# A two-layer kernel whose whole body is put into a block that the scheduler orders by a playback of time lines

## The chip, the core and the metric

The kernel runs on one core of one Trainium2 chip. The metric is the device time of one launch in microseconds. The time before is the median of 15 runs, 1619.65 us, with a lowest run of 1613.36 us and a highest of 1627.61 us.

## The reference, cut to what matters

The input is 8 sequences of 512 tokens with 128 features (4096 tokens). Two layers are computed. In each, the tokens are normalised, one branch `s` and one gate `g` are computed from the normalised tokens, and `x + s * silu(g)` goes on.

```python
xn = _layernorm(x)
s = _L0_attn_ref(xn, ...)   # a state-space block: convolution, scan over 512 steps, gating, MLP
g = _silu(_L0_ffn_ref(xn, ...))   # 24 experts, two matmuls with a layer norm between them
x = x + s * g
xn = _layernorm(x)
s = _L1_attn_ref(xn, ...)   # causal attention, 8 heads of 128
g = _silu(_L1_ffn_ref(xn, ...))   # 128 experts, one matmul each
x = x + s * g
```

The scan is `h = dA * h + dBx; y = h . C` over 512 steps, for 256 channels with 16 states each. The experts of both layers take the two best tokens' choices with a limited number of places; rows are moved to and from the experts by indirect DMAs. The second layer needs both branches of the first, sequence by sequence.

## The kernel before, in words

All of it is one function, `tile_kernel`, that traces about 10,000 instructions in program order. A list scheduler then decides the order on each engine: it walks through the traced instructions on a simulated machine and gives each engine, whenever it is free there, the ready instruction that comes first in program order. On the chip every engine then works through its own list in that fixed order; an instruction that waits holds back all that stand behind it on its engine. So the lists decide what may run beside what.

The work, in program order, with the names and lines that are used below:

- **prepare** (lines 230 to 282): for each sequence, layer norm, transposes, the router's logits and the running counts of the 24 experts. **routing** (lines 337 to 421) turns them into the places of the rows. The last step of it are the copies at lines 407 to 410, which hold the row numbers (`inv`) that the first expert gather needs.
- **expert1** (lines 439 to 455), 24 times: gather rows (`xg`), transpose, matmul (`ph`, line 453), scale, write to `hs_dram`.
- **between** (lines 457 to 504), 16 pairs of token tiles: gather four blocks (`hd`), add, layer norm (DVE lines 484 to 501), write to `hid_dram`.
- **expert2** (lines 506 to 522), 24 times: three gathers (`hg`), transposes (`pht`, line 515), matmul (`po`, line 520), scale, write to `os_dram`. Its first gather needs every row of `between`.
- **fetch** and **after** (lines 524 to 548): gather-add of `os_dram`, layer norm, gate; the input of the second layer for one sequence. The first of them needs every row of `expert2`.
- **front** (lines 551 to 586), **scan** (lines 591 to 632), **gate**, **back** (lines 635 to 704): the state-space block of one sequence. `scan` has 8 passes of two states each. Such a pass is called a *chunk* below; there are 64, numbered 0 to 63 through all sequences. A chunk is, for each half of the channels, two exponentials on ScalarE (ACT, line 603), a product on VectorE (DVE, line 605), two scans on DVE (line 607), a product on DVE (line 608), and 16 transposes on TensorE (PE, line 629) that add into PSUM. Its two broadcast loads (`bb`, `cb`, lines 597 and 598) are issued from ACT's queue.
- **Attention** (lines 743 to 914): `prepare` and `route` of one sequence, then `heads`, 8 passes. Such a pass is called a *head*; there are 64, numbered 0 to 63. Its scores are lines 849 to 864 (PE, a custom DVE reduction, an ACT exponential), its values lines 866 to 895 (transposes, a copy `pT` at line 879, matmul `po` at line 884, DVE sums at 893 and 895). The copies at lines 843 and 879 are written as `nc.any.tensor_copy`: the scheduler chooses DVE or ACT for each.
- **slots, experts, finish** (lines 954 to 998): the second layer's experts and the output.

In program order these parts are interleaved by hand: `step()` takes one chunk of the state-space block, and the calls of `step()` are spread over expert1, between, expert2 and the first 48 heads. Which chunk stands beside which expert or head on an engine is then the scheduler's choice. The PSUM pool `ps_m` (two buffers of tag `pm`) serves front, gate, back and, up to the end of the state-space block, the attention as well.

```python
    step()
    due = 0.0
    for n, of in mixture():
        due += n / of
        while due > 0.5:
            step()
            due -= 1.0
```

Of the kernel before, what the change touches and what calls it, by code (L numbers as in the profile page):

```python
# [42 lines left out]
)  # L43


@with_exitstack
def tile_kernel(ctx: ExitStack, tc: tile.TileContext, t: dict, out: bass.AP):
    nc = tc.nc
    V, S, G, T, Q = nc.vector, nc.scalar, nc.gpsimd, nc.tensor, nc.sync

# [5 lines left out]
    def load(src, shape, name, pool=None, dtype=F32):  # L56
# [11 lines left out]
        out=tri, in_=ones, pattern=[[1, P]], compare_op=ALU.is_gt, fill=0.0, base=0, channel_multiplier=-1  # L68
# [79 lines left out]
    def pool(stack, name, bufs, side, **more):  # L148
# [68 lines left out]
        out=group, in_=group, pattern=[[-B, H0]], compare_op=ALU.is_ge, fill=0.0, base=0, channel_multiplier=1  # L217
    )
    G.affine_select(
        out=group, in_=group, pattern=[[B, H0]], compare_op=ALU.is_ge, fill=0.0, base=B - 1, channel_multiplier=-1  # L220
# [3 lines left out]
        out=earlier, in_=earlier, pattern=[[-B, H0], [0, B]], compare_op=ALU.is_ge, fill=0.0, base=0,  # L224
# [438 lines left out]
    def back(b, yt):  # L663
# [49 lines left out]
        out=mask[:, L - P :], in_=mask[:, L - P :], pattern=[[-1, P]], compare_op=ALU.is_ge, fill=-FMAX,  # L713
# [512 lines left out]
```

## Time and profile before

| | |
|---|---|
| median of 15 runs | 1619.65 us |
| profiled execution, its own time | 1623.98 us |
| its span (first to last instruction) | 1622.3 us, so 1.7 us lie around it |
| DVE busy | 1257.7 us, 78% of the span |
| PE busy | 1233.2 us, 76% |
| ACT busy | 985.4 us, 61% |
| POOL (GpSimd) busy | 603.0 us, 37% |
| DMA | 222.76 MB, mean 137 GB/s |
| granted TensorE clock, mean | 0.873 |

The table is of the profiled execution, which is 4.3 us above the median. A busy share is the time in which the engine had at least one instruction in work, over the span. No engine is full on the average, so the order of the work in time matters beside its amount; the profile's busy shares over slices of time show where an engine is full.

### The profile page before, as it was taken

The numbers are of one execution on the slowest core, as the hardware profiler recorded it, in microseconds if no ns is written. First come the engines' busy times: TensorE is split into PE (matmuls) and PEld (weight loads), VectorE is DVE, ScalarE is ACT, GpSimd is POOL, SyncE is SP. The second block draws the span as 40 slices with busy tenths as digits, with TensorE's granted clock in tenths as the row PEclk, the third lists the DMA queues.
The fourth block names the chain that finished last, engine by engine and source line by source line (L and its number), as shares of the span: only waits on it lengthen the run. The fifth ranks groups of instructions, "written<-read, shape, count | busy, mean of one in ns | idle before, by whom it ended". The sixth has DMA issues, their size and how long they took to land.

```text
span 1622.3 us, 20522 instructions
## 1 busy us (share of the span) xinstructions
PE 1233.2 (76%) x6797; PEld 866.5 (53%) x6797; DVE 1257.7 (78%) x2831; ACT 985.4 (61%) x1696; POOL 603.0 (37%) x502
## 2 busy tenths in 40 slices
PE   4787989311388998254887898889979899898974
PEld 3653545101276886142465665666657667566743
DVE  6548686679856766695999999999999997475565
ACT  2226778566566786454677776767768665563363
POOL 2006763556283550723243503632430130210176
PEclk9887999655589999577798999989999999999987
DMA  5428987777567863423231321423211120058344
GB/s 139 152 95 295 308 284 234 225 234 246 166 214 235 264 198 136 112 77 85 72 107 46 104 90 34 114 77 97 63 57 66 53 71 1 28 148 240 94 111 122
DMA packets 170668, 222.76 MB, mean 137 GB/s; under 512 B 15722, under 2 KB 115898, under 8 KB 170562
## 3 DMA queue, kind: packets, MB, share of 16 engines
q1 hardware_dynamic: 125634, 101.35, 20.0%
q0 software_dynamic: 26496, 52.98, 12.4%
q10 hardware_dynamic: 18432, 67.12, 12.3%
q8 instruction: 54, 0.88, 0.2%
q14 instruction: 52, 0.43, 0.1%
HBM read 163.52 MB, written 57.80 MB: 136 GB/s over the span
## 4 chain that ended last, share of the span: by engine, by line
PE 34%; DVE 31%; DMA 12%; issue 9%; ACT 7%; POOL 6%; SPq 0%; ACTq 0%; POOLq 0%; DVEq 0%
DVE u L607 7%; PE sc L857 3%; PE po L884 3%; DVE u L605 3%; DVE u L608 3%; PE py L629 3%; DVE sc L859 3%; PE po L520 3%; PE ph L453 2%; DMA hd<-hs_dram,row 2%; DVE s L895 2%; PE pc L561 2%; POOL hd L127 2%; DVE pT L879 2%; PE pqm L849 1%
## 5 line engine op out<-in xcount | busy, mean ns | idle before, releaser
L607 DVE TENSOR_TENSOR_SCAN u<-da,u 128x512 f32<-128x512 f32 x256 | 311.1, 1235 | 68.8 <-ACT da L603 68.6
L629 PE MATMUL py<-ident,u 128*128 128x128 f32 x1024 | 170.2, 305 | 158.8 <-DVE u L608 158.6
L629 PEld LDWEIGHTS py<-ident,u 128*128 128x128 f32 x1024 | 135.4, 157 | 199.2 <-DVE u L608 177.2
L603 ACT ACTIVATE da<-dt,a_neg 128x512 f32<-128x512 f32 x256 | 175.7, 720 | 52.1 <-DVE u L607 49.7
L884 PE MATMUL po<-v,pT 128*128 128x129 f32 x1280 | 184.2, 286 | 23.8 <-DVE s L895 19.8
L884 PEld LDWEIGHTS po<-v,pT 128*128 128x128 f32 x1280 | 166.8, 198 | 56.1 <-issue 32.7
L863 ACT ACTIVATE prob<-sc,mn 128x128 f32<-128x128 f32 (+3 forms) x256 | 130.4, 527 | 98.4 <-DVE mn L859 90.6
L857 PE MATMUL sc<-xaT,qm 128*128 128x128 f32 (+3 forms) x512 | 179.5, 459 | 12.2 <-ACT prob L863 10.4
L605 DVE TENSOR_TENSOR u<-bb,lp 128x1024 f32<-128x1024 f32 x128 | 154.8, 1226 | 22.4 <-DMA bb<-xd_dram 16.7
L608 DVE TENSOR_TENSOR u<-u,cb 128x1024 f32<-128x1024 f32 x128 | 157.7, 1232 | 1.1
L859 DVE CUSTOM_DVE_ANT_0 sc<-sc,mask 128x128 f32<-128x128 f32 (+3 forms) x256 | 124.6, 494 | 31.9 <-PE sc L857 30.0
L127 POOL DMA_INDIRECT xg<-xn_dram,inv x72 | 98.0, 1361 | 121.5 <-DVE lp L584 79.4
L831 POOL DMA_INDIRECT xs_dram<-xn,idx x64 | 80.9, 1265 | 159.6 <-DVE idx L825 110.6
L877 PE MATMUL pp<-ident,prob 128*128 128x128 f32 x640 | 112.8, 284 | 27.3 <-DVE pT L879 21.6
L130 POOL DMA_INDIRECT o<-os_dram,row x64 | 113.7, 1776 | 47.6 <-DMA o<-xn_dram 29.8
L127 POOL DMA_INDIRECT hg<-hid_dram,inv x72 | 93.8, 1303 | 98.7 <-PE pht L515 48.5
L877 PEld LDWEIGHTS pp<-ident,prob 128*128 128x128 f32 x640 | 80.5, 145 | 89.2 <-issue 34.3
L857 PEld LDWEIGHTS sc<-xaT,qm 128*128 128x128 f32 x512 | 83.1, 198 | 50.3 <-ACT prob L863 28.4
L127 POOL DMA_INDIRECT hd<-hs_dram,row x64 | 76.0, 1188 | 76.6 <-DMA sb<-s_dram 30.8
L520 PE MATMUL po<-we,hgT 128*128 128x128 f32 x576 | 79.2, 286 | 0.3 <-ACT hgT L517 0.3
L520 PEld LDWEIGHTS po<-we,hgT 128*128 128x128 f32 x576 | 71.8, 198 | 11.8 <-issue 7.1
L849 PE MATMUL pqm<-xaT,m_qk 128*128 128x512 f32 x128 | 71.8, 652 | 4.5 <-DVE zm L701 1.9
(293 smaller groups left out, 2563.9 us busy)
## 6 DMA issues: line engine op xcount, KB each, us to landing
bb<-xd_dram ACTq DMA_DIRECT2D x64, 512.0 KB
cb<-xd_dram ACTq DMA_DIRECT2D x64, 512.0 KB
hs_dram<-hs SPq DMA_DIRECT2D x24, 768.0 KB
we<-in_W SPq DMA_DIRECT2D x48, 256.0 KB
hid_dram<-hd SPq DMA_DIRECT2D x32, 256.0 KB
we<-in_we SPq DMA_DIRECT2D x16, 512.0 KB
os_dram<-os SPq DMA_DIRECT2D x24, 192.0 KB
xb<-in_x SPq DMA_DIRECT2D x16, 256.0 KB
```

Of the source, the lines that this page charges most:

```text
L127: G.indirect_dma_start(dst, None, table[:, :], IOA(idx, 0))
L520: T.matmul(po[:, c, :], hT[:, f, :], we[:, f, :], start=False, stop=(f == NJ - 1))
L603: S.activation(da[:, j, :], dt[:, hf, :], AF.Exp, scale=a_neg[:, hf, n0 + j : n0 + j + 1])
L605: V.tensor_tensor(u, bb, bc(dx[:, hf : hf + 1, :], (P, NC, L)), ALU.mult)
L607: V.tensor_tensor_scan(u[:, j, :], da[:, j, :], u[:, j, :], 0.0, ALU.mult, ALU.add)
L608: V.tensor_tensor(u, u, cb, ALU.mult)
L629: T.matmul(py[:, i, hf * P : (hf + 1) * P], us[hf][:, j, i * P : (i + 1) * P], ident, is_transpose=True, start=False, stop=(n0 + j == DS - ...
L857: T.matmul(sc[:, :w], qm[:, i * P : w], xaT[:, :w], start=True, stop=True)
L859: V.tensor_tensor_reduce(sc[:, :w], sc[:, :w], mask[:, L - w :], -1.0, FMAX, ALU.add, ALU.min, mn[:, i : i + 1])
L863: S.activation(pr, sc[:, :w], AF.Exp, bias=mn[:, i : i + 1], scale=-1.0)
L877: T.transpose(pp[:, c, :], prob[i][:, k * P : (k + 1) * P], ident)
L884: T.matmul(po[:, i - i0, :], pT[:, i * (i + 1) // 2 + k, :], v[:, k, hd % 4, :], start=(k == 0), stop=(k == i),)
```

## The change

The old body of `tile_kernel` becomes a function `stages`, and `tile_kernel` calls it inside `tc.block(schedule_with_timeline_sim=True)`. The list scheduler then walks through the same traced instructions on another simulated machine, which plays back a time line for each engine and queue; so instructions become ready at other moments of that walk, and the lists come out in another order. Every tile and every computing instruction is the same; the engine of a `nc.any` copy is chosen anew.

```diff
+def tile_kernel(tc: tile.TileContext, t: dict, out: bass.AP):
+    with tc.block(schedule_with_timeline_sim=True):
+        stages(tc, t, out)
+
+
 @with_exitstack
-def tile_kernel(ctx: ExitStack, tc: tile.TileContext, t: dict, out: bass.AP):
+def stages(ctx: ExitStack, tc: tile.TileContext, t: dict, out: bass.AP):
     nc = tc.nc
```

Below, "the built order" is the list of instructions of each engine in the built program, before and after. Lines are those of the kernel before; in the changed kernel they are five higher.

## The prediction

> **What bounds the kernel now.** I read the page's busy shares over slices first, then the busy time of each engine by stage, then where the scans (line 607) and the attention matmuls (line 884) fall in these stages, and last the costliest groups. The page, with the engines' totals, slices, and the chain that ended last:
>
> ```profile
> PE 1233.2 (76%) x6797; PEld 866.5 (53%) x6797; DVE 1257.7 (78%) x2831; ACT 985.4 (61%) x1696; POOL 603.0 (37%) x502
> ...
> PE   4787989311388998254887898889979899898974
> ...
> DVE  6548686679856766695999999999999997475565
> ...
> PE 34%; DVE 31%; DMA 12%; issue 9%; ACT 7%; POOL 6%; SPq 0%; ACTq 0%; POOLq 0%; DVEq 0%
> ```
>
> DVE and PE have almost the same total, and neither is full. The slices show that they are full at different times, DVE from slice 20 to 33, PE in most others. Busy time by stage (window, length, then PE, PEld, DVE, ACT, POOL with instructions, granted clock, DMA share, GB/s):
>
> ```profile
> 0.00:133.00 133.00, 87.44 (x450) 59.66 (x450) 74.73 (x334) 34.08 (x53) 22.87 (x51) 0.85 0.48 147
> 133.00:313.00 180.00, 151.19 (x612) 83.86 (x612) 136.47 (x142) 130.47 (x212) 105.43 (x80) 0.91 0.82 269
> 313.00:440.00 127.00, 25.89 (x112) 21.08 (x112) 107.49 (x185) 78.51 (x126) 59.24 (x50) 0.52 0.68 216
> 440.00:650.00 210.00, 184.19 (x1329) 155.71 (x1330) 139.79 (x139) 150.87 (x287) 96.45 (x75) 0.93 0.65 207
> 650.00:811.00 161.00, 82.48 (x339) 51.57 (x337) 124.32 (x195) 85.03 (x130) 63.22 (x42) 0.71 0.32 87
> 811.00:1347.00 536.00, 476.43 (x2589) 333.84 (x2587) 513.76 (x1294) 377.53 (x653) 174.04 (x120) 0.95 0.25 74
> 1347.00:1423.00 76.00, 70.64 (x387) 48.67 (x386) 43.15 (x149) 40.79 (x82) 9.17 (x11) 0.98 0.10 29
> 1423.00:1622.00 199.00, 154.90 (x988) 112.11 (x986) 118.01 (x401) 88.07 (x156) 72.64 (x75) 0.90 0.51 140
> ```
>
> The stages are: start, expert1, between, expert2, the step to the first head, heads with scan, heads alone, tail. In the longest one, 811 to 1347, DVE is busy 513.76 of 536 us and PE 476.43: both are nearly full because scans and attention run beside each other. The same windows for the scans of line 607 alone (DVE busy, count) and the matmuls of line 884 alone (PE, PEld):
>
> ```profile
> 440.00:650.00 210.00, 61.88 (x52) 0.93 0.65 207
> ...
> 811.00:1347.00 536.00, 118.84 (x96) 0.95 0.25 74
> ```
> ```profile
> 811.00:1347.00 536.00, 120.06 (x841) 109.18 (x842) 0.95 0.25 74
> ```
>
> A chunk has four such scans, so 13 chunks lie beside expert2 and 24 beside the heads. The groups that price this:
>
> ```profile
> L607 DVE TENSOR_TENSOR_SCAN u<-da,u 128x512 f32<-128x512 f32 x256 | 311.1, 1235 | 68.8 <-ACT da L603 68.6
> L605 DVE TENSOR_TENSOR u<-bb,lp 128x1024 f32<-128x1024 f32 x128 | 154.8, 1226 | 22.4 <-DMA bb<-xd_dram 16.7
> L608 DVE TENSOR_TENSOR u<-u,cb 128x1024 f32<-128x1024 f32 x128 | 157.7, 1232 | 1.1
> L127 POOL DMA_INDIRECT hg<-hid_dram,inv x72 | 93.8, 1303 | 98.7 <-PE pht L515 48.5
> L879 DVE COPY pT<-pp 128x512 f32<-128x512 f32 x31 | 21.1, 680 | 2.4 <-PE pp L877 2.1
> L879 ACT COPY pT<-pp 128x384 f32<-128x384 f32 x60 | 28.7, 478 | 25.7 <-PE pp L877 25.4
> ```
>
> A chunk costs DVE (311.1 + 154.8 + 157.7) / 64 = 9.7 us.
>
> **How I price an order.** Nothing computes less, so I count what stands where in the built order after, and give each instruction the mean busy time of its group (line, shape, engine) in the trace before, overlap with its predecessor left out. Summed over the old order this gives back the page's totals. In a stage where engines feed each other, the time is at least the largest engine sum of the stage. Check on the old order: from head 0 to head 63, head by head, the largest sums add to 781 us; the trace has 790 (811 to 1601). Over the four stages from 133 to 811 us they add to about 155 + 121 + 197 + 128 = 601, against 678 (113%).
>
> **Part 1, the block itself.** The built program has one more branch on no engine and no barrier in the body: priced at nothing. At most it is one more wait of all engines; the 1.7 us around the span bounds that.
>
> **Part 2, the copies.** Of the `nc.any` copies DVE keeps 29 instead of 130 and ACT does 227 instead of 126. DVE loses 28 v copies at 682 ns, 53 pT of 384 columns at 545 and 20 of 512 at 680: 61.6 us, 55 without overlap. ACT gains 28 at 588, 53 at 478, 20 at 586: 53.5 us, and loses 32 of its 202 table loads at 1283 ns: 41 us; net 12. On a DVE-bound stretch the 55 us would be gain; the end values are 0 and -55.
>
> Taken alone, the Trainium skill (Perfetto Trace Analysis, Identifying the Most-Contended Engine) says to take the engine of highest occupancy, here DVE, and relieve that first; by it the profiled time would be 1624 - 55 = 1569 us. The same page (Optimization Strategy) says that a kernel whose most-contended engine changes over time can gain from interleaving these regimes; by it an order that parts them loses, and the rest of this text measures how much.
>
> **Part 3, the scan runs ahead of the experts.** In the old order, expert 0's matmul (line 453) stands beside chunk 1 and the last of expert1 beside chunk 11; between lies beside chunks 13 to 17, expert2 beside 18 to 30. In the new order DVE is done with chunk 0 after 61 us of work instead of 79, and routing is strewn among chunks: its last copy (line 408) stands behind 231 us of DVE work, at chunk 15. So expert1 runs beside chunks 16 to 31, between starts at chunk 34, and after chunk 39 the lists hold no scan until the first attention preparation: nine of the 16 pairs of between, then all 720 PE instructions of expert2 in one row, are alone. Front's second half for sequence 5, without which chunk 40 cannot start, stands behind that preparation. Stage by stage:
>
> - Chunk 0 done: 133 us before, of which DVE works 75; 18 us of DVE work and 16 us of PE work now stand behind it, and both fed it: 115.
> - Chunks 1 to 15 with prepare and routing: DVE 170 us. Chunks 0 to 4 ran at 97% in the trace, so 1.07 times: 182, to 297.
> - Expert1 with chunks 16 to 31: PE 180, DVE 175, ACT 154. Three full engines that feed each other had 180/155 before; I take 1.1: 198, to 495.
> - Chunks 32 to 39 and seven pairs: DVE 119, times 1.07: 128, to 623.
> - Nine pairs alone: DVE has 37 us, but the first eight pairs took 59 us in the trace with DVE not full (four gathers and two stores each), 7.4 a pair: 66, to 689.
> - Expert2 alone: PE 112 us, POOL 72 gathers at 1.303 = 94. Lead-in of the first gather 12, then 118: 819. DVE and ACT's scan work, 140 us of DVE in the old stage, is not there: this is the loss.
> - Fetch, after, preparation to head 0: 161 us before, with 124 of DVE work in it, and about 48 from preparation to head 0 alone. Now 8 gather-adds at 1.86 apart, then the chain: 60, to 879.
>
> Head 0 thus comes at about 879 us instead of 811, with the same 40 chunks done: +68.
>
> **Part 4, scans and heads part.** From there the old order has the last 24 chunks spread over 42 heads. In the new one chunks 40 to 47 stand beside heads 0 to 3, none beside heads 4 to 14, 48 to 55 beside 15 to 17, none to 28, 56 to 63 beside 28 to 31, none from there on. Largest sums: 95 (DVE), 139 (PE; DVE 81), 77 (DVE), 127 (PE; DVE 87), 72 (DVE), 148 (PE, heads 31 to 48). That is 658, where the old order needed 1423 - 811 = 612 in all; at 107% it is 704. The tail from head 48 has the same work as before: 199. Together 903. Head by head the largest sums are 865 against 781, which by the check is 875 from head 0 to 63, plus 21 after it: 896. So +85 to +92 here, the 55 us of Part 2 already in.
>
> **Part 5, other queues.** SP: fetch 0's load of `s_dram` now stands ahead of routing's copies to `inv` and waits for back 0; back 0 ends by chunk 12, `inv` needs chunk 15, so that hides it; if not, each us goes to expert 0. ACT issues the 128 loads of `bb` and `cb`; waits for `bb` were 16.7 us in all and lie in the 1.07; from none to one of the 7 us landings seen at some chunks, for each of the three bursts' eight, it is 0 to 168, and I stay at the row's 16.7. POOL's gathers keep their order, with two 1.28 us additions of back moved past.
>
> **Sum.** 879 + 896 = 1775, with the 1.7 around it 1777, less 4.3 (profiled run to median) 1772. Without any friction it is 115 + 170 + 180 + 119 + 66 + 112 + 60 = 822 to head 0 and 658 + 199 = 857 after it, or 835 if engines may drift by two heads: 1655 to 1677. Windows of four heads give 786 us for the new order and 727 for the old, so 786 x 790/727 + 21 = 875 after head 0 and 1751 in all. I take 1755.
>
> **Rivals.** (a) DVE's relief decides: the bursts hide, buffers let PE run past them, and the stretch 811 to 1347 falls to PE's 476 us at 97%, 490: 46 us less, 1575 us, faster. For it: DVE 96% busy there. Against: head 4's DVE instructions stand behind chunk 47 in one list. It wins only while head 0 comes less than 46 us late and the heads stay beside the scans. Chance 0.06. (b) The engines drift more than I allow, at or just under the frictionless sum: 1640 to 1677. Chance 0.14. (c) A queue blocks: loads at the burst starts, or an SP wait ahead of `inv`: 50 to 168 us on top, 1820 to 1930. Chance 0.1. (d) The order hardly changes, so no change: the built orders differ in over 4000 lines on PE, so 0.02. Forecast: 0.68.
>
> **How the numbers follow.** About 0.2% (3 us) is what a measurement can tell from no change. Faster: (a) and nothing else, 0.06; same: (d) and the edge between, 0.03; slower 0.91. The range leaves out (a), (d) and the upper part of (c), and reaches to (b): 1645 to 1845.
>
> **What would show it.** In the profile after: scans (x count of line 607) absent while line 520 runs, DVE near zero there for about 120 us; expert1 starting near 290 us; head 0 near 870 us; DVE copies at 879 down to 26; three DVE-full bursts between PE-full stretches. It is wrong if expert2 ends before 720 us, or if heads 0 to 63 take under 800 us.

## The result and the profile after

The changed kernel takes 1760.47 us (median of 9 runs, 1756.83 to 1766.91) against 1619.65 us (47 runs): a ratio of 1.0872, 95% interval 1.0853 to 1.0891, so 141 us slower. The forecast was 1755 us. The span of the profiled execution is 1759.2 us, the mean granted clock 0.843 against 0.873. Lines of the changed kernel are five higher than those named so far.

The page after, in the same lines as shown of before (totals, slices, chain):

```profile
PE 1249.8 (71%) x6797; PEld 890.3 (51%) x6797; DVE 1218.6 (69%) x2730; ACT 991.9 (56%) x1765; POOL 607.3 (35%) x502
...
PE   5863588989844119933666889669778799989960
...
DVE  7499998979798750004889637995388967455663
...
PE 14%; DVE 8%; ACT 4%; issue 4%; POOL 3%; DMA 2%; ACTq 0%; DVEq 0%; SPq 0%; POOLq 0%
```

The work is nearly the same: PE has 17 us more (1%), DVE 39 us less (3%). What is new is in the slices: three zeros in DVE's row at slices 16 to 18, and further on dips (6, 3, 5, 3) where DVE had nines. The chain holds 35% of the span only, so nothing is read from it. Busy time by stage (length, then PE, PEld, DVE, ACT, POOL with instructions, granted clock, DMA share, GB/s):

```profile
95.00:287.00 192.00, 115.34 (x599) 89.60 (x600) 182.77 (x238) 90.10 (x135) 34.41 (x14) 0.68 0.38 126
...
650.00:765.00 115.00, 110.12 (x936) 104.35 (x936) 0.00 (x0) 63.26 (x144) 66.22 (x70) 0.97 0.79 249
765.00:861.00 96.00, 31.25 (x76) 13.82 (x77) 40.87 (x127) 34.36 (x54) 79.02 (x59) 0.57 0.31 59
861.00:960.00 99.00, 63.17 (x299) 47.56 (x298) 89.58 (x192) 65.55 (x114) 40.53 (x22) 0.79 0.30 78
960.00:1090.00 130.00, 112.87 (x590) 76.80 (x589) 77.14 (x247) 80.08 (x140) 35.99 (x33) 0.95 0.18 50
1090.00:1185.00 95.00, 66.48 (x343) 45.78 (x341) 93.41 (x154) 55.01 (x108) 0.13 (x1) 0.89 0.21 72
1185.00:1307.00 122.00, 104.83 (x528) 69.13 (x529) 68.36 (x239) 73.23 (x138) 26.80 (x23) 0.93 0.16 42
1307.00:1409.00 102.00, 80.07 (x406) 56.28 (x405) 93.79 (x160) 72.34 (x129) 10.72 (x10) 0.87 0.21 70
1409.00:1554.00 145.00, 135.40 (x801) 99.31 (x800) 87.37 (x337) 91.33 (x176) 20.42 (x25) 1.00 0.14 40
```

The first line is DVE full with scans while no expert has begun. The second is expert2 with no DVE instruction at all; the third is the step to head 0. Then bursts of scans (DVE 90 of 99 us, PE 63) take turns with stretches of heads (PE 113 of 130, DVE 77). Head 0 stands here at its first value matmul (line 884): 811 us before, 861 now. For the kernels of the experiments it is its first sum (line 889), which comes 1 to 6 us later.

The granted clock is lower, but it cannot hold the loss: after head 0 PE is busy 705 us at a clock of 0.90 against 702 us at 0.94, so its work takes 3 us longer there, where the part itself grows from 811 to 898 us; in the whole kernel PE has 17 us more, against 137 us of span (before, then after):

```profile
811.00:1620.00 809.00, 701.97 (x3961) 494.62 (x3958) 674.92 (x1842) 506.39 (x890) 255.85 (x206) 0.94 0.30 86
```
```profile
861.00:1759.00 898.00, 704.99 (x3949) 501.92 (x3947) 625.14 (x1715) 524.17 (x966) 206.80 (x188) 0.90 0.26 73
```

The scans alone (line 612) from 861 us on, and the longest DVE wait between 640 and 870 us (total, times, longest):

```profile
861.00:960.00 99.00, 27.80 (x24) 0.79 0.30 78
960.00:1090.00 130.00, 9.29 (x8) 0.95 0.18 50
1090.00:1185.00 95.00, 37.22 (x32) 0.89 0.21 72
1185.00:1307.00 122.00, 0.00 (x0) 0.93 0.16 42
```
```profile
DVE lno_st L111 <- DMA o<-os_dram,row: 159.5, 13, 141.1
```

DVE stands once for 141.1 us: the layer norm of `after` heads its list and waits for rows that exist only when expert2 is done. The group of the scans:

```profile
L612 DVE TENSOR_TENSOR_SCAN u<-da,u 128x512 f32<-128x512 f32 x256 | 300.4, 1213 | 0.2
```
A scan costs what it did (1213 ns, 1235 before). Its engine waits for it less, 0.2 us against 68.8. In turn ACT, whose exponentials feed the scans, now waits 127.8 us for DVE's scans (49.7 before): the scans stand in blocks in which DVE is the late one, and between these blocks DVE has none.

### The profile page after: what moved, and what is told of

Its sections match the earlier page's. It is cut to its first block, busy times and chain, and to the rows that moved or that the text cites. A ratio compares the mean times of both kernels' runs of the same rounds, so it can differ in the third digit from the quotient of the medians.

```text
span 1759.2 us, 20610 instructions
## 1 busy us (share of the span) xinstructions
PE 1249.8 (71%) x6797; PEld 890.3 (51%) x6797; DVE 1218.6 (69%) x2730; ACT 991.9 (56%) x1765; POOL 607.3 (35%) x502
## 5 line engine op out<-in xcount | busy, mean ns | idle before, releaser
L612 DVE TENSOR_TENSOR_SCAN u<-da,u 128x512 f32<-128x512 f32 x256 | 300.4, 1213 | 0.2
L608 ACT ACTIVATE da<-dt,a_neg 128x512 f32<-128x512 f32 x256 | 170.5, 714 | 152.0 <-DVE u L612 127.8
L862 PE MATMUL sc<-xaT,qm 128*128 128x128 f32 (+3 forms) x512 | 197.2, 480 | 53.2 <-ACT prob L868 49.8
L634 PEld LDWEIGHTS py<-ident,u 128*128 128x128 f32 x1024 | 148.2, 171 | 169.7 <-DVE u L613 146.2
L132 POOL DMA_INDIRECT xg<-xn_dram,inv x72 | 127.7, 1774 | 81.5 <-DVE lp L589 32.5
L111 DVE BATCH_NORM_STATS2 lno_st<-o 128x6 f32<-128x128 f32 x32 | 9.3, 292 | 189.2 <-DMA o<-os_dram,row 189.1
L135 POOL DMA_INDIRECT o<-os_dram,row x64 | 105.8, 1654 | 51.3 <-DMA os_dram<-os 20.2
L882 PE MATMUL pp<-ident,prob 128*128 128x128 f32 x640 | 110.1, 283 | 15.2 <-ACT pT L884 10.8
L884 ACT COPY pT<-pp 128x384 f32<-128x384 f32 (+1 forms) x166 | 85.0, 512 | 63.7 <-PE pp L882 49.9
L132 POOL DMA_INDIRECT hd<-hs_dram,row x64 | 85.8, 1341 | 81.3 <-DVE u L612 22.4
L704 POOL TENSOR_TENSOR zm<-zm,b 128x512 f32<-128x512 f32 x8 | 33.0, 4121 | 229.2 <-PE pzt L690 160.2
L836 POOL DMA_INDIRECT xs_dram<-xn,idx x64 | 67.7, 1058 | 106.0 <-DVE row L833 84.0
```

The lines of the kernel that those rows point to most:

```text
L132: G.indirect_dma_start(dst, None, table[:, :], IOA(idx, 0))
L135: G.indirect_dma_start(dst, None, table[:, :], IOA(idx, 0), compute_op=ALU.add)
L608: S.activation(da[:, j, :], dt[:, hf, :], AF.Exp, scale=a_neg[:, hf, n0 + j : n0 + j + 1])
L612: V.tensor_tensor_scan(u[:, j, :], da[:, j, :], u[:, j, :], 0.0, ALU.mult, ALU.add)
L634: T.matmul(py[:, i, hf * P : (hf + 1) * P], us[hf][:, j, i * P : (i + 1) * P], ident, is_transpose=True, start=False, stop=(n0 + j == DS - ...
L862: T.matmul(sc[:, :w], qm[:, i * P : w], xaT[:, :w], start=True, stop=True)
```

## The experiments

The twelve kernels ran on three chips on which the kernel before has medians of 1640.93, 1641.05 and 1643.13 us, 1.3 to 1.5% above the 1619.65; so each result is read by its ratio to before on the same chip. Stage times come from one profile each, and against the two profiles above they carry that percent.

### The block alone

```diff
+def tile_kernel(tc: tile.TileContext, t: dict, out: bass.AP):
+    with tc.block():
+        stages(tc, t, out)
```

> The body in a block, but ordered as before, without the playback of time lines; the built order is the same as before on every engine, with one more branch. If the lost time comes from the order alone: 1620 us, within 4 us of before. If the block itself costs (a barrier, a branch, another start): up to the 1760 us of the changed kernel.

Measured: 1641.86 us, ratio 1.0003 (0.9968 to 1.0038). Without the playback the built lists are the old ones on every engine, and the time is the old one. All of the loss comes from what the playback changes: the lists, and the engines of the copies.

### Holding one instruction per chunk in program order

The first: from the end of expert2 on, the first product of each chunk and the first reduction of each head on DVE. The second: up to the end of expert2, the first transpose of each chunk on PE. The third: both.

```diff
-                V.tensor_tensor(u, bb, bc(dx[:, hf : hf + 1, :], (P, NC, L)), ALU.mult)
+                m = V.tensor_tensor(u, bb, bc(dx[:, hf : hf + 1, :], (P, NC, L)), ALU.mult)
+                if pin["dve"] and hf == 0:
+                    tc.keep_in_program_order(m)
...
+                        if pin["pe"] and hf == 0 and j == 0 and i == 0:
+                            tc.keep_in_program_order(m)
...
+                if pin["dve"] and i == 0:
+                    tc.keep_in_program_order(m)
```

> The changed kernel, but from the end of expert2 on the first DVE product of each chunk and the first DVE reduction of each head are held in program order on DVE, so that the remaining chunks are spread over heads 0 to 48 again. Experts and chunks before are left as changed (expert2 still alone, beside no chunk). Theory (two separate losses, experts late and scans parted from heads): head 0 stays near 860 us, the rest falls from 898 to about 820 to 840, 1680 to 1705 us. Rival (the time after head 0 is set by the sum of work and the copies on ACT, not by the spread): no change, 1750 to 1765 us. Rival (all of the loss is the late experts): no change either, with head 0 at 860.

> The changed kernel, but up to the end of expert2 the first PE transpose of each chunk is held in program order on PE, so that a chunk stands beside the expert it was written beside (expert 0 beside chunk 1, expert2 beside chunks 17 to 30). Scans and heads stay parted as changed. Theory: head 0 falls from 861 to about 810 to 825 us, the rest stays near 898, 1707 to 1725 us. Rival (the loss is the parting of scans and heads alone; the wait in expert2 costs nothing since the same 40 chunks are done): 1755 to 1765 us. Rival (all of the loss is the late experts): 1620 to 1640 us.

> Both holds at once: chunks beside their experts on PE, and beside their heads on DVE; the copies stay mostly on ACT (19 on DVE instead of 130 before). Theory: both losses go, 1620 to 1650 us; if the 60 us of copies taken off DVE are worth something in the DVE-full stretch, 1590 to 1615. Rival (something else in the order costs, such as POOL, SP or ACT's queue): above 1660 us.

Measured: ratios of 1.126 (1.1201 to 1.1319), 1.0988 (1.0926 to 1.1049) and 1.12 (1.1146 to 1.1254). Each hold made the changed kernel slower, so the two theories failed; of the third expectation its rival is left, that something else in the order costs. The second did bring expert1 forward, to 183 us from 287, and head 0 still came late, at 901. DVE's waits in the second, from 95 to 352 us, and in the first, from 888 to 1573 us:

```profile
DVE u L612 <- PE py L638: 69.7, 7, 28.2
```
```profile
DVE rsum L902 <- PE po L897: 57.8, 40, 6.2
```

In the second, the product of a chunk (line 605, here 612) waits for late transposes on PE, which have to read a buffer before it is written again. In the first, a sum of attention heads DVE's list while PE has not made its product. That wait is not new: it is 50.5 us in the changed kernel (861 to 1554) and 8.7 in the kernel before (811 to 1427). The hold did spread the scans, 12 to 16 in each 100 us from 888 to 1488 (15 to 21 in the kernel before), and the part after head 0 still takes 956 us: scans spread on DVE's list alone don't bring the time back. The third run has both sides of this: expert1 begins at 182 us, head 0 comes at 893, and the part after it takes 948. A chunk's first instruction was put back, while the playback ordered its partners on the other engines by its own time lines. So "chunks stand at the wrong heads" is not the whole cause; which list stands against which must be asked.

### One order up to head 0, the other after it

Here both programs' built lists are written into the kernel before, as a chain on every engine, and the engine of each copy as a letter. One kernel takes the old lists up to the first attention matmul (line 849) and the new ones from there, the other the reverse.

```diff
+    copies = iter(COPIES)
...
-                nc.any.tensor_copy(pT[:, first : first + n, :], pp[:, :n, :])
+                copy(pT[:, first : first + n, :], pp[:, :n, :])
...
+        for a, b in zip(places, places[1:]):
+            tc.add_manual_dep(
+                traced[b], traced[a].name,
+                mybir.DependencyInfo(mybir.DependencyClass.NoSync, mybir.DependencyReason.DATA),
+                reason="order",
+            )
```

> Every engine runs the kernel before's order up to the first attention head (copies on the same engines as there), and the changed kernel's order from there on. Two separate losses (theory A): head 0 where the kernel before has it, about 811 us, and after it the 898 us of the changed kernel: about 1710 us against 1620, some 5.5% more than before. One loss only at the front, the attention being slow because it starts late (theory B): after it about 811 us, the whole within 1.5% of before. The order is not what matters but the number of instructions and waits the frame makes (theory C): no clear figure, but both this kernel and its opposite would then be alike.

> Every engine runs the changed kernel's order up to the first attention head, and the kernel before's order from there on. Theory A: head 0 at about 861 us and then 811 us: about 1672 us against 1620, some 3% more than before. Theory B (the late front costs the attention too): 861 + 898, as the changed kernel, some 8.5% more. Theory C: as its opposite.

Measured: old then new 1.0753 (1.0696 to 1.081); new then old 1.0315 (1.0262 to 1.0368). Theory A stands in its main point: there are two separate losses, and each comes from the order (with its choice of engines for the copies). Busy time by stage of "new then old" (its lines are 20 above before's), then of "old then new" after head 0:

```profile
650.00:874.00 224.00, 147.70 (x1024) 122.09 (x1022) 44.59 (x141) 100.00 (x202) 137.06 (x123) 0.79 0.53 147
874.00:1689.00 815.00, 692.48 (x3928) 488.67 (x3928) 661.02 (x1799) 488.32 (x870) 231.80 (x191) 0.94 0.29 82
```
```profile
858.00:1766.00 908.00, 706.52 (x3927) 503.40 (x3927) 622.62 (x1701) 520.20 (x962) 204.12 (x187) 0.90 0.25 72
```

With the old lists the part after head 0 takes 815 us though it starts 63 us later (811 in the kernel before); with the new ones it takes 908 even with the old lists ahead of it (898 in the changed kernel). "Old then new" is 2 points dearer than expected, because its head 0 comes at 858 and not at 811: at the seam the new lists begin with gather-adds for later sequences, and from 811 to 858 POOL is busy 34 us, DVE 18. The two parts therefore don't add exactly (7.5 + 3.1 against 8.7%).

### One engine's list alone put back

The same chain for DVE alone, or PE alone, in the changed kernel, with the old engines for the copies; the playback makes the other lists anew, so these are neither the old ones nor those of the changed kernel.

> The changed kernel with VectorE's list alone held in the kernel before's order (and the copies on the same engines as there); the other engines' lists are again made by the playback. If VectorE's list decides (theory V), nearly all of the 141 us comes back: within 2% of before, about 1620 to 1650 us. If TensorE's list decides (theory P), most of the loss stays: 6% or more above before. If the loss is in the pairing of the two lists (theory W), it stays or is larger than in the changed kernel, since a list from one order runs against lists of another.

> The changed kernel with TensorE's list alone held in the kernel before's order (and the copies on the same engines as there). Theory V (VectorE's list decides): most of the loss stays, 6% or more above before. Theory P (TensorE's list decides): within 2% of before. Theory W (the pairing): as the changed kernel or slower.

Measured: DVE's old list 1.0767 (1.0696 to 1.0838), PE's old list 1.1257 (1.1182 to 1.1332). Neither engine's old list brings the time back by itself (theories V and P fall); DVE's gives back one point of 8.7, PE's makes it worse. From head 0 to the end (832 to 1763 us) DVE's old list waits for heads that the playback's PE list makes too late:

```profile
DVE sc L880 <- PE sc L878: 86.1, 76, 4.1
DVE rsum L910 <- PE po L905: 66.2, 39, 3.9
```

In the kernel before these two waits are 30.0 and 22.2 us from 811 us on, in the changed kernel 59.4 and 66.6 from 861 on. That agrees with theory W: in-order engines that feed each other need lists that fit each other.

### The copies alone, in either order

The chain again: the old order with the changed kernel's copy engines, and the new order with the old ones. The edit is the string of letters only.

> The kernel before's order held on every engine; only the engine of each copy of v and pT is the changed kernel's (101 fewer on VectorE, as many more on ScalarE, each at its old place in the common order). If VectorE's time bounds the attention part (theory R, relief), about 55 us less VectorE work in a stretch where it is over nine tenths busy: 1.5 to 3% less than before. If the copies only move a wait, since TensorE's next products wait for pT wherever it is copied (theory N), within 1%.

> The changed kernel's order held on every engine, with the kernel before's engines for the copies (101 more on VectorE). Theory R: the relief is worth its 55 us in the changed kernel too, and without it the time is 11 to 12% over before. Theory N: it is worth nothing there, since scans and heads lie apart and VectorE has room beside the heads: 8 to 9.5% over before, as the changed kernel.

Measured: 1.0044 (1.0015 to 1.0072) and 1.1008 (1.0977 to 1.1039). In the old order the relief of DVE by way of ACT is worth nothing; the chain is in these 0.4% too. The stretch that was 811 to 1347 before, with less to do for DVE, and DVE's waits in it, then the same wait in the kernel before:

```profile
818.00:1355.00 537.00, 474.02 (x2571) 329.50 (x2568) 471.25 (x1208) 406.80 (x728) 167.39 (x120) 0.96 0.25 74
```
```profile
DVE sc L879 <- PE sc L877: 30.0, 45, 3.3
```
```profile
DVE sc L859 <- PE sc L857: 8.8, 21, 2.2
```

DVE's work falls from 513.76 to 471.25 us and the stretch stays, 536 and 537 us: the time became waits for PE, the one shown from 8.8 to 30.0 us, the one for the attention sums (line 889) from 0.2 to 10.8. At 96% busy DVE's work was not by itself what set the length. What did is open: PE's busy time stays too (476 and 474 us), and PE now waits 18 us for copies on ACT where it waited 3.4 for those and 7.3 for copies on DVE, so a part of the relief may be paid there. In the new order the relief does help: without it the ratio is 1.1008 instead of 1.0872, some 22 us (1.36% of 1620, from ratios on two chips), and the part after head 0 takes 927 us against 898 (some 12 us of that are the slower chip's percent). It fits that DVE bounds in the bursts (90 of 99 us busy); where the 22 us fall was not measured apart.

### Filling DVE beside expert2

The order of "new then old", with chunks 32 to 39 taken out of their place ahead of expert2 and spread over expert2's instructions on every engine.

> The order of the run that took the changed kernel's order up to head 0 and the kernel before's after it (that run: 3.1% over before), with one stretch altered: chunks 32 to 39 are taken out of the stretch before expert 2 and spread over expert 2's own instructions. If the loss ahead of head 0 is that VectorE stands empty beside expert 2 (theory U, unfilled), the stretch before expert 2 shrinks from 133 us to some 100 (16 pairs at about 6 us each) and expert 2 stays near 115 us: head 0 some 30 us earlier, 1 to 2% over before. If the pairs and expert 2 have a pace of their own that the scans slow when beside them (theory O), nothing comes back: 3 to 4% over before.

Measured: 1.0375 (1.0342 to 1.0409), not better than the 1.0315 without the filling; theory O. The pairs of between did finish earlier, and expert2 began at 604 us instead of 650. But with eight chunks beside it expert2's matmuls (line 520) took 177 us (604 to 781) where "new then old" has 120 (650 to 770), and head 0 came at 883 against 874:

```profile
600.00:780.00 180.00, 152.16 (x1159) 137.78 (x1160) 79.52 (x77) 107.47 (x216) 91.75 (x73) 0.92 0.70 222
```

Empty time on DVE beside expert2 is therefore not, by itself, what costs the 50 us ahead of head 0: PE, which does expert2's products and the scans' transposes both, is busy 152 of these 180 us. Whether PE's pace or the waits between the lists stretch expert2 was not separated.

### Bursts in the old kernel

The kernel before, without block or playback, with one loop altered: 24 chunks that were spread over 48 heads come in three bursts.

```diff
+    BURSTS = (3, 17, 30)
...
-        while (taken - (NSTEP - left)) * total < (i + 1) * left:
-            step()
+        if i in BURSTS:
+            while (taken - (NSTEP - left)) * len(BURSTS) < (BURSTS.index(i) + 1) * left:
+                step()
```

> The kernel before, with one loop altered: the 24 chunks that it spreads evenly over 48 heads are taken in three bursts of eight, after heads 3, 17 and 30, as the changed kernel has them; block, playback and the rest are not used. If scans and heads lying apart is what costs the 87 us after head 0 (theory S, apart), 40 to 97 us more than before, that is 2.5 to 6% (the frame's own order still pulls some chunks out of the bursts). If what costs is something else in the played-back lists, such as the place of single instructions (theory F), within 1% of before.

Measured: 1698.20 us (its profiled run is 11 us above that), 1.0316 (1.0281 to 1.0351), 52 us slower: theory S, within its bounds and near their lower end. The scans (line 607) by 50 us in this kernel, then in the kernel before:

```profile
850.00:900.00 50.00, 21.47 (x19) 0.83 0.27 90
1000.00:1050.00 50.00, 4.86 (x4) 0.97 0.24 60
1050.00:1100.00 50.00, 15.37 (x12) 0.97 0.28 73
1200.00:1250.00 50.00, 7.31 (x6) 0.90 0.11 35
```
```profile
850.00:900.00 50.00, 11.92 (x10) 0.90 0.21 61
1000.00:1050.00 50.00, 10.82 (x8) 0.97 0.37 97
```

What was 8 to 12 scans in each 50 us from 850 to 1350 became 4 to 19. Ahead of the heads nothing moved: head 0's first sum comes at 818.1 us here and at 819.6 in the run of the block alone, which has the old lists and a median within 2 us of before's here (813.7 in the faster profile of before); all of the loss lies after it. Counted from that first sum on, DVE's built list changes between scan instructions (lines 605 to 608) and head instructions (lines 849 to 895) 256 times before, 170 times here and 138 times in the changed kernel; the parts from there on take 809, 890 and 896 us in the profiles (the 890 on the slower chip and with the 11 us in it; the block alone has 825). DVE's count alone does not give the time: with DVE's old list alone (above) it is 238, but PE's list changes only 98 times between transposes of chunks (line 629) and heads, against 134 before, and that part takes 931 us.

## Why the prediction was right, and where not

**Direction, place and total.** Two losses were forecast, both from order: +68 us ahead of head 0 and +85 to +92 after it. The profile has +50 and +87, and the mixed kernels show that each comes from the order. That the total came within 5 us is in part luck: the stages added up to 1772, 1755 was chosen between that and 1751, and below errors of 30 to 50 us cancel in both parts. What was named as signs came: no scan while expert2 runs, DVE at 0.00 us for 115, expert1 at 287 (290), head 0 at 861 (870), 26 DVE copies of `pT`, bursts of scans.

**Part 1, the block at nothing.** Shown: 1.0003.

**Part 2, the copies.** The 55 us were counted whole, inside the sums of the part after head 0. DVE's busy time fell by 39 us in all, and the relief is worth some 22 us (by the ratios) in the new order and none in the old. Rival (a) rested on them alone: it took the 96% of DVE for a bound, and the old order with the new copies refutes that, 0.4% slower where 46 us were to be won. The rule quoted from the Trainium skill (Perfetto Trace Analysis, Identifying the Most-Contended Engine) would have won 55 us by the prediction's reading; measured, with the copies moved to ACT in the old order, is a loss of 7 us (0.44% of 1643). What the same page says in Optimization Strategy, that kernels whose most-contended engine changes over time can gain from interleaving, agrees with the bursts: taking the interleaving away cost 52 us.

**Part 3, ahead of head 0: right by two errors.** Every stage up to expert2 but one was priced too long, and chunks 1 to 15 too short (192 us measured, 182 priced; the 97% quoted for its friction would give 1.03, not 1.07). Chunk 0 was done at 95 us (115), the last expert of expert1 began at 469 (end forecast at 495), the pairs were done at 650 (689), expert2 at 765 (819). The terms that were off are the first stage's 20 us and the friction: 10% on expert1, 7.4 us for a pair alone (the last ten pairs, behind the last scan at 587 us, took 6 us each), 118 and 12 us for expert2, where 115 us in all were measured. The step to head 0 then took 96 us instead of 60. There 15 us of gather-adds and 48 of preparation were named, which alone make more than the 60. And the count of gather-adds failed: eight were priced, and POOL's list has 16 in a row ahead of the first product of `after`, since the second sequence's fetch also stands there (start, length, idle before):

```profile
767.41 1.59 POOL L135 DMA_INDIRECT o<-os_dram,row  x1 [20.19 <-DMA os_dram<-os]
...
795.33 1.55 POOL L135 DMA_INDIRECT o<-os_dram,row  x1 [0.30 <-issue]
796.31 1.86 POOL L547 TENSOR_TENSOR o<-o,lno_w 128x512 f32<-128x512 f32 x1
```

That is 29 us instead of 15. With 2 us ahead of it, 9 for the four operations of `after` on POOL (796 to 805) and 56 for the preparation (48 priced) it makes up the 96. Together -54 and +36: head 0 at 861, 18 us earlier than forecast; that the two nearly cancel is luck. The name of that part's loss, "140 us of DVE in the old stage is not there", was argued, not shown, and putting 80 us of it back gained nothing; what costs these 50 us stays open.

**Part 4, after head 0.** 896 was forecast as 875 and 21; measured is 898 as 845 and 53, so that -30 and +32 cancel, with the tail at 205 (199). The bursts took 99, 95 and 102 us where the sums times 1.07 were 102, 82 and 77, so the friction was too small in the last two; the stretches of heads took 130, 122 and 145 against 149, 136 and 158, so it was too large there. The sum held; its parts were each up to 25 us off. That parting costs is shown: bursts alone, in the old kernel, cost 46 to 58 us, where the changed kernel loses 87 after head 0. The rest is not separated: the changed kernel parts harder (138 alternations on DVE against 170), and single instructions stand elsewhere too.

**Part 5 and rival (c).** No queue blocked: DVE's idle time ahead of the products that read `bb` is 2.5 us in all, of which 2.4 end with PE (before, 16.7 us ended with a load). **Rival (b)**, 1640 to 1677, would have had engines drift past the bursts; a profile with 90 of 99 us DVE in a burst and 113 of 130 us PE after it speaks for engines bound in turn. **Rival (d)** was given 0.02 with a count of 4000 differing lines. That count says little, as every line number had moved by five. Matched by instruction, 47 of 4722 matmuls on PE and 3 of 2735 instructions on DVE stand at their old place in the list; the conclusion holds by that.

**Open.** What exactly makes head 0 50 us late in the new order; the trace puts some 15 us of it on the second sequence's eight gather-adds, which no run took away. Bringing expert1 forward by a hold on PE did not help, nor did filling expert2; both disturbed other lists. None of the kernels was faster than the kernel before.

## What to carry to other kernels

When two kinds of work bound different engines, count in the built lists how often they alternate on each engine: bursts of the one and stretches of the other move the time toward the sum of their bounds; here three bursts of eight chunks cost 52 us. A busy share of 96% does not say that less work on that engine shortens the stretch; take the work away and see whether the time turns into waits. And lists belong together: a single engine's good list, or one held instruction in each chunk, run against lists from another order gave back one point of 8.7 at best (1.0767) and else cost more than the bad order (1.0988 to 1.126).

## What the runs showed of the hardware that was not expected

The same kernel took 1619.65 us in the first comparison, whose chip is not on record, and 1640.93 to 1643.13 us on the three chips of the experiments, 1.3 to 1.5% more. That is more than some effects measured here, so they are compared by ratios on one chip. And beside an empty DVE and ACT at half load, expert2's 24 experts ran at 115 us for 110 us of PE work, a friction of 4%, where the stages with three busy engines needed 13% over their largest sum in the kernel before.
